# The four projections of u: four 32-column matmuls in place of one 128-column matmul

## The chip, the cores and the metric

One core of one Trainium2 chip. The metric is the device time of one execution in microseconds. The kernel before was timed in two runs: 3685.1 and 3701.43 us, median 3693.26 us.

## The reference

The input x is (4, 128, 96, 96): four images, 128 channels, fp32. Each is group-normalised (32 groups), read as a sequence of 9216 pixels in four orders (rows, rows backwards, columns, columns backwards), and each sequence goes through a gated state-space scan. The four results are put back into pixel order, mixed by `fuse_w`, and added to x. Cut to what matters here, for one sequence:

```python
t = grouped1x1(x, in_proj_w, in_proj_b, 4)         # 128 -> 512 channels, 4 groups of 32
u, gate = t[:, :256], t[:, 256:]
u = depthwise_conv(silu(u), dw_w)                  # 5 taps along the sequence
s = conv1x1(u, ssm_in_w)                           # 256 -> 32, and so are the next three
a = 0.999 + 0.0009 * sigmoid(conv1x1(u, ssm_delta_w, ssm_delta_b))
b = tanh(conv1x1(u, ssm_b_w, ssm_b_b))
c = tanh(conv1x1(u, ssm_c_w, ssm_c_b))
prefix = cumsum(log(clip(a, 0.0001, 0.9999)))
h = exp(prefix) * cumsum(b * s * exp(-prefix))
u = u + conv1x1(c * h + d * s, ssm_out_w)          # 32 -> 256
y = out_proj(grouped1x1(u * sigmoid(gate), mix_w, mix_b, 4))
```

The four projections of u are s, b, c and a's argument (delta): 32 channels each, together 128.

## The kernel before

Each image has two phases: V (pixels taken by columns) and H (by rows). In a phase silu(in_proj(groupnorm(x))) lies whole in SBUF, and two passes go over it, one for each direction. A pass walks 20 chunks of whole lines: 18 of 5 lines (480 pixels) and 2 of 3 lines (288 pixels). 4 images x 2 phases x 2 passes x 20 chunks make 320 steps, and all of it is fp32.

A step has these pieces, by function and line:

- `conv_and_gate`: the depthwise convolution. Channels 0 to 127 on TensorE as five matmuls with diagonal weights (L249, tile pc, copied to u by ScalarE at L265); channels 128 to 255 on ScalarE (first tap, L260) and VectorE (four taps, L262). Then the gate: two matmuls with 32 rows each (L271, tile pg, on rows 64 to 95 and 96 to 127), and their sigmoid (L275, tile gv).
- `scan`: the projections pp of u (L288), one matmul with 128 output columns for each half of u's channels, the second half (j = 1) first. The weights are laid out s, b, c, delta in groups of 32 columns, so that the result's partitions 0 to 31 hold s, 32 to 63 b, 64 to 95 c and 96 to 127 delta. ScalarE takes tanh of b (L293, tb), sigmoid of delta (L295, a) and tanh of c (L299, z); GpSimd scales and clips a (L301, L302); VectorE multiplies b and s (L303), runs the recurrence (L309, h), and makes z (L318, L319).
- `ssm_out`: z goes through two matmuls with 32 rows (L325 into pc, L329 into pz), and VectorE adds and gates (L330 to L332).
- `accumulate`: the folded output weights times gv (L340, tile py, two 128x128 matmuls), added to acc by VectorE (L345 in phase V).
- `front`: for the chunks of the next phase, during the second pass of a phase: normalisation, two matmuls with 32 rows (L225, tile pu, on rows 0 to 31 and 32 to 63), sigmoid (L229) and silu (L232).

The loop at the end runs the steps with one step's distance: `conv_and_gate` of step n, `ssm_out` of step n-1, `front` of a chunk where one is due, `scan` of step n, `accumulate` of step n-1. The framework keeps roughly this order on each engine, moves some instructions in the first chunks, and sets the waits from the data that instructions share. Each engine works through its own queue in that order. Tiles u, gv, tb, a, z and h have two buffers each, as do pc (`ps_u`) and pp (`ps_p`) in PSUM; pz and py have one.

So an ordinary step of the first pass stands in TensorE's queue as: L249 (5 matmuls), L271 (2), L325, L329, L288 (2), L340 (2). In second passes the two of L225 stand between L329 and L288.

## Time and profile before

| | |
|---|---|
| runs | 3685.1 and 3701.43 us, median 3693.26 |
| profiled execution: its span, first to last instruction | 3681.5 us (the page gives no other time for it; the runs lie 3.6 and 19.9 us above) |
| TensorE matmuls, busy | 3543.3 us, 9032 records |
| TensorE weight loads, busy | 1550.5 us, 9032 records |
| VectorE, busy | 2937.6 us |
| ScalarE, busy | 1572.0 us |
| GpSimd, busy | 393.2 us |
| mean granted clock of TensorE | 0.938 |
| DMA over the span | 25 GB/s |

How to read it: PE is TensorE's matmuls, PEld its weight loads, which overlap them; DVE is VectorE, ACT ScalarE, POOL GpSimd. A group in the page is one source line on one engine: the output tile, the tiles it reads, the count, then busy time in us and the mean length of one in ns, then the idle time of the engine just before those instructions and what ended most of it. A timeline row is start in us, length in us, engine, line, operation, tiles, count, and in brackets the idle time ahead and its releaser. The ends of matmuls are modelled, so distances between starts tell more than lengths. PEclk is the share of TensorE's full clock that was granted.

### The profile page before, as it was taken

To read this page: it belongs to the slowest core of one execution; us is meant where nothing else is said; L and a number is where in the kernel's file an instruction comes from. 1 tells how busy PE (TensorE), PEld (TensorE's weight loads), DVE (VectorE), ACT (ScalarE), POOL (GpSimd) and SP (SyncE) were. 2 spreads that over 40 slices of the span, in tenths; PEclk is the share of its full clock that TensorE was granted. 3 is DMA by queue.
4 is the path that set the end of the run, shared out by engine and by line. 5 is a ranking of instruction groups with operands and counts; after the bars stand their busy time and mean duration, and the time that the engine had idled before them with its cause. 6 is when DMAs were issued, how large, how long until landed. Compare 5 with 4: busy or idle time off the path is not lost.

```text
span 3681.5 us, 27637 instructions
## 1 busy us (share of the span) xinstructions
PE 3543.3 (96%) x9032; PEld 1550.5 (42%) x9032; DVE 2937.6 (80%) x4442; ACT 1572.0 (43%) x2572; POOL 393.2 (11%) x653
## 2 busy tenths in 40 slices
PE   7999999999999999999999999999999999999999
PEld 3334444444443444444443444444444344444444
DVE  7788887788877888778887788777887778877777
ACT  3334444444443444444443444444444444444443
POOL 0011111111111111111111011111111111111111
PEclk8899999999999999999999999999999999999999
DMA  4210000002100000001210000000121000000000
GB/s 145 82 37 12 19 22 0 0 30 65 59 3 0 17 19 17 0 0 46 65 45 0 0 20 22 11 0 3 59 62 32 0 4 21 22 6 0 3 24 25
DMA packets 56625, 92.14 MB, mean 25 GB/s; under 512 B 7296, under 2 KB 56352, under 8 KB 56480
## 3 DMA queue, kind: packets, MB, share of 16 engines
q1 hardware_dynamic: 54720, 89.68, 8.0%
q8 instruction: 70, 1.15, 0.1%
q10 hardware_dynamic: 1760, 0.70, 0.1%
q14 instruction: 75, 0.61, 0.1%
HBM read 71.48 MB, written 18.87 MB: 25 GB/s over the span
## 4 chain that ended last, share of the span: by engine, by line
DVE 46%; PE 41%; issue 6%; ACT 4%; DMA 2%; POOL 0%; ACTq 0%; DVEq 0%; POOLq 0%
DVE u L262 12%; PE pp L288 8%; PE pc L325 8%; PE pc L249 8%; DVE h L309 8%; PE py L340 6%; PE pz L329 6%; DVE z L319 5%; DVE tb L303 4%; DVE z L318 4%; DVE gv L332 3%; PE pu L225 3%; DVE u L331 3%; DVE sil L232 3%; ACT u L260 2%
## 5 line engine op out<-in xcount | busy, mean ns | idle before, releaser
L249 PE MATMUL pc<-sil,diag 128*128 128x480 f32 (+1 forms) x3200 | 1299.5, 552 | 0.0
L262 DVE SCALAR_TENSOR_TENSOR u<-sil,w_dw,u 128x480 f32<-128x480 f32 (+1 forms) x1280 | 889.0, 695 | 135.4 <-ACT u L260 124.0
L249 PEld LDWEIGHTS pc<-sil,diag 128*128 128x128 f32 x3200 | 610.7, 191 | 643.3 <-issue 624.7
L288 PE MATMUL pp<-u,w_proj 128*128 128x480 f32 (+1 forms) x1280 | 705.2, 680 | 3.1 <-DVE u L262 2.0
L265 ACT COPY u<-pc 128x480 f32<-128x480 f32 (+1 forms) x320 | 173.8, 543 | 1074.9 <-PE pc L249 1074.8
L340 PE MATMUL py<-gv,w_fin 128*128 128x480 f32 (+1 forms) x1280 | 614.2, 605 | 0.9
L301 POOL TENSOR_SCALAR a<-a 32x480 f32<-32x480 f32 (+1 forms) x320 | 189.8, 593 | 3252.3 <-ACT a L295 3252.3
L330 DVE TENSOR_TENSOR gv<-pc,gv 128x480 f32<-128x480 f32 (+1 forms) x320 | 203.8, 637 | 343.5 <-PE pc L325 337.1
L275 ACT ACTIVATE gv<-pg,b_in 128x480 f32<-128x480 f32 (+1 forms) x640 | 379.2, 642 | 143.8 <-PE pg L271 133.4
L325 PE MATMUL pc<-z,w_so 32*128 32x480 f32 (+1 forms) x640 | 332.6, 599 | 101.8 <-DVE z L319 100.5
L340 PEld LDWEIGHTS py<-gv,w_fin 128*128 128x128 f32 x1280 | 282.6, 222 | 331.4 <-issue 234.6
L288 PEld LDWEIGHTS pp<-u,w_proj 128*128 128x128 f32 x1280 | 244.3, 212 | 390.2 <-issue 273.8
L260 ACT ACTIVATE u<-sil,w_dw 128x480 f32<-128x480 f32 (+1 forms) x320 | 216.8, 678 | 404.7 <-DVE gv L332 398.0
L309 DVE TENSOR_TENSOR_SCAN h<-a,h,tb 32x480 f32<-32x480 f32 (+1 forms) x304 | 354.7, 1167 | 1.1
L271 PE MATMUL pg<-xn,w_in 32*128 32x480 f32 (+1 forms) x1280 | 345.5, 600 | 0.6 <-ACT gv L275 0.6
L229 ACT ACTIVATE sg<-pu,b_in 128x480 f32<-128x480 f32 (+1 forms) x320 | 201.7, 638 | 274.8 <-PE pu L225 274.7
L329 PE MATMUL pz<-z,w_so 32*128 32x480 f32 (+1 forms) x640 | 301.1, 550 | 0.0
L225 PE MATMUL pu<-xn,w_in 32*128 32x480 f32 (+1 forms) x640 | 264.2, 632 | 9.1 <-DVE sil L232 7.7
L293 ACT ACTIVATE tb<-pp,b_proj 32x480 f32<-32x480 f32 (+1 forms) x320 | 204.0, 637 | 150.8 <-PE pp L288 145.1
L303 DVE TENSOR_TENSOR tb<-pp,tb 32x480 f32<-32x480 f32 (+1 forms) x320 | 198.9, 621 | 70.3 <-ACT z L299 67.3
L232 DVE SCALAR_TENSOR_TENSOR sil<-pu,b_in,sg 128x480 f32<-128x480 f32 (+1 forms) x320 | 219.0, 691 | 24.9 <-ACT sg L229 23.5
L331 DVE TENSOR_TENSOR u<-pz,u 128x480 f32<-128x480 f32 (+1 forms) x320 | 203.9, 637 | 43.7 <-PE pz L329 2.6
(54 smaller groups left out, 2122.3 us busy)
## 6 DMA issues: line engine op xcount, KB each, us to landing
xn<-in_xv SPq DMA_DIRECT2D x72, 240.0 KB, 2.6
acc<-in_xh SPq DMA_DIRECT2D x72, 240.0 KB, 2.8
xn<-in_xh SPq DMA_DIRECT2D x72, 240.0 KB, 2.6
out<-res SPq DMA_DIRECT2D x72, 240.0 KB, 2.0
xs<-in_xh SPq DMA_DIRECT2D x54, 240.0 KB, 2.6
xn<-in_xv SPq DMA_DIRECT2D x8, 144.0 KB, 2.4
acc<-in_xh SPq DMA_DIRECT2D x8, 144.0 KB, 2.4
xn<-in_xh SPq DMA_DIRECT2D x8, 144.0 KB, 2.1
```

What stands on the lines that cost most here:

```text
L225: nc.tensor.matmul(pt[:, :n], w_in[q, :], xn[q, span(c)], start=True, stop=True)
L232: nc.vector.scalar_tensor_tensor(sil[:, j, bass.ds(PAD + STARTS[c] * WW, n)], pts[j][:, :n], b_in[:, j : j + 1], sg[:, :n], ALU.add, ALU.mult,
L249: nc.tensor.matmul(pu[:, :n], diag[:, w, :], sil[:, 0, bass.ds(o + k, n)], start=(k == 0), stop=(k == K - 1),)
L262: nc.vector.scalar_tensor_tensor(u[:, 1, :n], src, coef, u[:, 1, :n], ALU.mult, ALU.add)
L271: nc.tensor.matmul(pg[:, :n], w_in[q, :], xn[q, span(c)], start=True, stop=True)
L275: nc.scalar.activation(gv[:, j, :n], pgs[j][:, :n], AF.Sigmoid, bias=b_in[:, 2 + j : 3 + j])
L288: nc.tensor.matmul(pp[:, :n], w_proj[:, j, :], u[:, j, :n], start=(j == 1), stop=(j == 0))
L303: nc.vector.tensor_mul(tb[:, :n], s, tb[:, :n])
L309: nc.vector.tensor_tensor_scan(dirn(h), dirn(a), dirn(tb), 0.0 if st["first"] else carry[0], ALU.mult, ALU.add,)
L325: nc.tensor.matmul(pu[:, :n], w_so[:, 0:P], z[:, :n], start=False, stop=True, skip_group_check=True)
L329: nc.tensor.matmul(pz[:, :n], w_so[:, P:HID], z[:, :n], start=True, stop=True)
L340: nc.tensor.matmul(py[:, :n], w_fin[:, d, j, :], gv[:, j, :n], start=(j == 0), stop=(j == 1))
```

## The change

In `scan`, the one matmul for each half of u's channels becomes four, one for each group of 32 output columns. Each reads the same u (128 partitions, all pixels of the chunk), its own 32 columns of the weights, and writes its own 32 partitions of pp. In the built program such a matmul is placed on a tile of 128 rows by 32 columns of the array, at column 0, 32, 64 or 96. The order is: half 1 with its four tiles, then half 0 with its four tiles. `skip_group_check` switches off a check of the framework on the start and stop flags of groups that share a PSUM bank. Comments were taken out as well; from the changed place on, a line of the changed kernel has a number higher by 7.

```diff
         for j in (1, 0):
-            nc.tensor.matmul(
-                pp[:, :n], w_proj[:, j, :], u[:, j, :n], start=(j == 1), stop=(j == 0)
-            )
+            for q in range(4):
+                r = slice(MH * q, MH * (q + 1))
+                nc.tensor.matmul(
+                    pp[r, :n],
+                    w_proj[:, j, r],
+                    u[:, j, :n],
+                    start=(j == 1),
+                    stop=(j == 0),
+                    skip_group_check=True,
+                )
```

## The prediction

> **What bounds the kernel now.** I read the page from the shares down, then its chain, then the instructions of one step, then who waits for whom. On the page:

> ```profile
> PE 3543.3 (96%) x9032; PEld 1550.5 (42%) x9032; DVE 2937.6 (80%) x4442; ACT 1572.0 (43%) x2572; POOL 393.2 (11%) x653
> ...
> PEclk8899999999999999999999999999999999999999
> ...
> DVE 46%; PE 41%; issue 6%; ACT 4%; DMA 2%; POOL 0%; ACTq 0%; DVEq 0%; POOLq 0%
> ...
> L288 PE MATMUL pp<-u,w_proj 128*128 128x480 f32 (+1 forms) x1280 | 705.2, 680 | 3.1 <-DVE u L262 2.0
> ...
> L325 PE MATMUL pc<-z,w_so 32*128 32x480 f32 (+1 forms) x640 | 332.6, 599 | 101.8 <-DVE z L319 100.5
> ```

> TensorE is busy 96% of the 3681.5 us span, and the only idle time worth naming ahead of a matmul is 101.8 us before L325, until VectorE's z (L319). TensorE sets the pace, VectorE follows closely (80%, and 46% of the chain, because the chain hops over to it at each z). L288, the line that changes, has 1280 records for 320 chunks x 2 halves: an fp32 matmul leaves two, each with a weight load of its own. I call them its two passes. One ordinary step in the timeline of TensorE:

> ```profile
> 2010.67 4.19 PE L249 MATMUL pc<-sil,diag 128*128 128x480 f32 x10
> 2014.79 1.07 PE L271 MATMUL pg<-xn,w_in 32*128 32x480 f32 x4
> 2016.17 1.07 PE L325 MATMUL pc<-z,w_so 32*128 32x480 f32 x2 [0.31 <-DVE z L319]
> 2017.08 0.96 PE L329 MATMUL pz<-z,w_so 32*128 32x480 f32 x2
> 2017.97 1.88 PE L288 MATMUL pp<-u,w_proj 128*128 128x480 f32 x4
> 2019.69 1.77 PE L340 MATMUL py<-gv,w_fin 128*128 128x480 f32 x4
> 2021.30 2.98 PE L249 MATMUL pc<-sil,diag 128*128 128x480 f32 x7
> ```

> Ends are modelled, so I use starts. py's four passes run from 2019.69 to 2021.30: 1.61 us, 0.4025 a pass. pp's four take 1.72 (2017.97 to 2019.69), 0.11 over that; pz's two take 0.89, 0.085 over theirs. So going from the 32-row tiles of pz to the whole array costs 0.085 us ahead of the first pass and 0.11 behind its start, where its weight load isn't hidden: 0.195 us a change of tile shape.

> **Two tiles do run at once.** pg is two 32-row matmuls, on rows 64 to 95 and 96 to 127. Its instructions in the window from 2014.5 to 2015.0, and in that from 2015.5 to 2015.8:

> ```profile
> L271 PE MATMUL pg<-xn,w_in x2: 665/665/665, 2014.8 to 2014.8; 32*128 32x480 f32 x2
> ```

> ```profile
> L271 PE MATMUL pg<-xn,w_in x2: 561/561/561, 2015.3 to 2015.3; 32*128 32x480 f32 x2
> ```

> Two passes start together, and 0.5 us later the other two. The built program has each matmul's two passes one behind the other, first matmul complete before the second; so the second tile's first pass overtook the first tile's second pass. Four passes took two slots.

> **The clock is a second bound.** The table by stretches of time:

> ```profile
> 2003.40:2006.80 3.40, 2.96 (x7) 1.39 (x8) 2.06 (x4) 1.16 (x2) 0.00 (x0) 0.97 0.00 0
> 2006.80:2010.20 3.40, 3.40 (x5) 1.39 (x5) 1.74 (x3) 2.50 (x4) 0.44 (x1) 0.53 0.01 2
> ```

> PEclk (third from the right) is about half in the second stretch, behind one that held the z wait and four quarter-height passes. I cut the trace into stretches of 3.413 us at the clock's own changes, and in each summed the passes, weighted by the rows they use (32 of 128 counts a quarter). Full-clock stretches followed by half clock, 98 of them, had at most 0.39 of the array in use; the 924 others at least 0.37, and 5% of them under 0.44. About 0.38 is the limit. 119 of 1043 stretches run at half, some 203 us lost. This decides what an inefficient pp would cost.

> [...]

> **The change, part by part.** Each 128-column matmul becomes four of 32 columns over all 128 rows and all 480 pixels; in the built program they carry tile shape 128x32 at columns 0, 32, 64, 96, so the change does what it says. Records go from 9032 to 12872. A 32-column pass streams the same 480 columns, so it costs 0.4025 us too: the array work can at best stay equal, four tiles at once.
> 1. Passes. If four tiles overlap as pg's two do: 2 halves x 2 passes x 0.4025 = 1.61 us, as before: 0. Not shown for columns; the bounds are the rivals below.
> 2. Entry. Before, pp is entered by a shape change (from pz or, in second passes, from L225's 32-row tiles); after, also: 0. Its exposed load is 32 columns, not 128: if the four load side by side the 0.11 falls to an estimated 0.03 [...], if in turn it stays. 0 to -26 us over 320; I take -13.
> 3. Exit. New: py behind pp was the same shape, now it is another: +0.195 x 320 = +62 us at full clock, /0.938 (mean clock) = +66.
> 4. Cover. The exit's drain lies behind pp's end, and z's work starts at pp's end (tanh and sigmoid L293 to L299, L301/L302, the scan), so where PE then waits for z the drain comes out of that wait: up to 0.195 x 230 waits = 45 us. But acc (L345) needs py and stands in VectorE's queue ahead of tb (L303); where it comes late, tb, scan and z do too and the cover is gone (0). I take -22.
> 5. Clock. A gap of 0.195 us in 3.413 lowers the use by up to 0.057; stretches between 0.38 and 0.44 then fall under the limit, at most 5% of 924, some 40, at half of 3.413, 1.7 us, each: 0 to +68; I take +34.
> 6. Waits and queues. The first tile of each half carries the wait on u, the fourth raises the count for itself and its neighbours; L293 waits for the fourth, as it waited for the whole. Nothing new waits. PE's queue gets 32 instructions (loads and passes) for pp instead of 8; pg's two first passes start 7 ns apart in the trace's records, so I cost their issue at 0. Without that cover the staggered rival's price below bounds it. ScalarE, GpSimd and the DMA queues keep their order; VectorE's moves slightly in the first chunks alone: 0. The longer program adds 0.5 MB of instructions to 25 GB/s: hidden, DMA engines are idle most of the time.

> Sum: -13 + 66 - 22 + 34 = +65 us on 3681.5, span 3746.5. The runs' median is 3693.3, 11.8 above that span, so 3758 us (+1.8%). All low ends: -26 + 66 - 45 = -5; all high: +134. Own range of this case 3700 to 3830. It straddles 2% (3767), about what a measurement of this kernel can tell from no change.

> **The rivals.**
> Staggered or half rate (22%). Columns share the rows; if passes issue in program order, each tile's second pass blocks the next tile, 9 slots instead of 4: 9 x 0.4025 = 3.62 us, +2.01. If four streams of u from the same partitions get half the rate: +1.61. With 32 of 320 steps narrower (288 pixels) the mean is 0.96 of it: +495 to +617 us, with the exit 4250 to 4380. The array is then in use 0.45 to 0.5 in pp, beside a stretch at 0.25: about one more half-clock stretch a step, 320 x 1.7 = +545: to 4900, more where half begets half: 5400. For: [...] fp32 has two passes a tile. Against: pg's overtaking.

> Serial, the case on the other side (13%). Tiles of one row group don't overlap at all: 16 x 0.4025 = 6.44, +4.83 x 0.96 x 320 = +1480, 5240; at 0.25 of the array for 8 us a step at least two stretches go half, +1090: 6300. It decides from a second pass slot on: one extra slot of 0.4 us a half is already +247 us, 6.7%. [...]

> Dear changes of shape (5%): if a column shape's switch costs three times the row shape's, +125 more: 3880.

> Faster (3%): if the clock's limiter counted four small passes as more work than one large, the 203 us of half clock go: 3540. Nothing in the trace says so; otherwise no term is negative enough.

> **How the numbers follow.** Likeliest 57%: 3758. About 0.42 of it lies over 3767: 0.24, with the slow rivals' 0.40 makes slower 0.64; same 0.33; faster 0.03. Range for 8 in 10: from 3700 (leaves out faster and the likeliest's low tail, some 0.06) up to 5400, which takes in staggered and half rate with the clock's share, and leaves out most of serial (0.12).

> **What will show it.** Right: four L288 passes starting within some ns of each other, pp from first start to py's first start about 1.8 us, a gap of some 0.09 before py and 0.11 behind its first pass, mean clock 0.92 to 0.94, z wait below 100 us. Wrong: L288 passes 0.4 us apart one by one (serial), pairs in a staircase (staggered), passes 0.8 us apart (half rate), or a mean clock under 0.85.

## The result, and the profile after

The changed kernel takes 3716.46 us (3713.41 to 3719.51, two runs) against 3693.26: 1.0063 of before, interval 1.0034 to 1.0092. Run again beside other kernels it took 1.0077 (1.0063 to 1.0091). The forecast of 3758 us gave the direction, but +65 us became +23 to +28. One of all the runs below, of the kernel before with three TensorE taps, took 16293 us, and neither its time nor its profile is used.

The page of the changed kernel: engine shares, granted clock, chain, and two groups (the last column is the idle time ahead).

```profile
PE 3603.4 (97%) x12872; PEld 1417.5 (38%) x12872; DVE 2950.2 (79%) x4442; ACT 1571.7 (42%) x2572; POOL 393.0 (11%) x653
...
PEclk8899989999999998999999999899999999899999
...
PE 61%; DVE 32%; issue 4%; ACT 2%; DMA 2%; ACTq 0%; SPq 0%; DVEq 0%
...
L290 PE MATMUL pp<-u,w_proj 128*32 128x480 f32 (+1 forms) x5120 | 698.9, 663 | 2.0 <-DVE u L262 2.0
...
L332 PE MATMUL pc<-z,w_so 32*128 32x480 f32 (+1 forms) x640 | 332.9, 599 | 79.6 <-DVE z L326 75.6
```

pp has four times the passes and no more busy time (698.9 us): the tiles overlap. The idle time before z's matmul fell from 101.8 to 79.6 us, so some of the change went into a wait that was there anyway. (The 128-column matmul had 705.2 us of busy time, in the prediction's lines.) The step that answers to the one shown in the prediction, in the timeline of TensorE:

```profile
2013.67 0.96 PE L336 MATMUL pz<-z,w_so 32*128 32x480 f32 x2
2014.57 1.82 PE L290 MATMUL pp<-u,w_proj 128*32 128x480 f32 x16
2016.32 1.88 PE L347 MATMUL py<-gv,w_fin 128*128 128x480 f32 x4
2018.03 1.37 PE L249 MATMUL pc<-sil,diag 128*128 128x480 f32 x3
```

pp to py is 1.75 us (1.72 before), py to the taps 1.71 (1.61 before). In pp's records within 2014.5 to 2014.9, and within 2015.2 to 2015.38, four passes start together each time:

```profile
L290 PE MATMUL pp<-u,w_proj x4: 590/590/590, 2014.6 to 2014.6; 128*32 128x480 f32 x4
```

```profile
L290 PE MATMUL pp<-u,w_proj x4: 566/566/566, 2015.0 to 2015.0; 128*32 128x480 f32 x4
```

The records have the four 7 ns apart, all first passes, then all second passes, though the program lists each tile's two passes together. Over all steps at full clock, from starts (medians), two gaps are new. From pp's last pass to py's first it is 0.496 us, 0.093 over a pass; I call that drain, though the records show its length and not what fills it. From py's first pass to its second it is 0.507, 0.104 over a pass; I call that exposed load, since py's first weight load starts with the first pass (2016.313 and 2016.315 us in this step) and not in an earlier one. pp's exposed load fell by 0.08, and the tiles' spacing adds 0.02. That is 0.137 us more TensorE time a step, 44 us over 320 steps: what steps 2 and 3 of the prediction said, to 9 us. But the kernel became slower by less than that.

### What sets a step

I measured each step from one start of L303 (tb's product on VectorE) to the next. In first passes at full clock the median step is 10.50 us in the H order and 10.83 in the V order, before and after alike. z's last instruction in three first-pass steps of the kernel before, then two of the changed kernel:

```profile
2442.45 0.70 DVE L319 SCALAR_TENSOR_TENSOR z<-pp,d_sb,z 32x480 f32<-32x480 f32 x1
2452.94 0.70 DVE L319 SCALAR_TENSOR_TENSOR z<-pp,d_sb,z 32x480 f32<-32x480 f32 x1
2463.44 0.70 DVE L319 SCALAR_TENSOR_TENSOR z<-pp,d_sb,z 32x480 f32<-32x480 f32 x1
```

```profile
2476.92 0.70 DVE L326 SCALAR_TENSOR_TENSOR z<-pp,d_sb,z 32x480 f32<-32x480 f32 x1
2487.42 0.70 DVE L326 SCALAR_TENSOR_TENSOR z<-pp,d_sb,z 32x480 f32<-32x480 f32 x1
```

The same 10.50, with 0.137 us more on TensorE. The chain of the kernel before shows why (start, length, who; a V-order step):

```profile
2016.17 1.07 PE pc L325 x2
2017.24 0.82 PE pz L329 x2
2018.08 0.67 DVE u L331
2018.77 0.67 DVE gv L332
2019.52 0.70 ACT u L260
2020.25 0.73 DVE u L262
2021.00 0.72 DVE u L262
2021.72 0.99 DVE acc L345
...
2026.23 0.72 DVE z L319
```

From z through two short matmuls to VectorE, over to ScalarE's first tap (it waits for u's buffer: 398.0 of the 404.7 us that ScalarE idles before L260 end with VectorE's L332), back to VectorE's taps, acc, tb, scan and z: this loop holds neither pp nor the taps on TensorE. The share of 96% hid that TensorE has slack in the first-pass steps that run at full clock.

**A second edit nobody wrote.** In the built programs VectorE's queue differs in some 105 steps of second passes: the framework's scheduler turned `tb, acc, scan, tap, z` into `acc, tb, tap, scan, z` (res stands for acc where the result is written out). A second-pass step before, then one of the changed kernel, in VectorE's timeline:

```profile
1735.49 0.64 DVE L303 TENSOR_TENSOR tb<-pp,tb 32x480 f32<-32x480 f32 x1
1736.06 0.70 DVE L354 SCALAR_TENSOR_TENSOR res<-py,b_fin,acc 128x480 f32<-128x480 f32 x1
1736.68 1.20 DVE L309 TENSOR_TENSOR_SCAN h<-a,h,tb 32x480 f32<-32x480 f32 x1
1737.81 0.68 DVE L262 SCALAR_TENSOR_TENSOR u<-sil,w_dw,u 128x480 f32<-128x480 f32 x1
1738.42 0.64 DVE L318 TENSOR_TENSOR z<-z,h 32x480 f32<-32x480 f32 x1
```

```profile
1741.93 0.71 DVE L361 SCALAR_TENSOR_TENSOR res<-py,b_fin,acc 128x480 f32<-128x480 f32 x1
1742.55 0.63 DVE L310 TENSOR_TENSOR tb<-pp,tb 32x480 f32<-32x480 f32 x1
1743.12 0.70 DVE L262 SCALAR_TENSOR_TENSOR u<-sil,w_dw,u 128x480 f32<-128x480 f32 x1
1743.74 1.20 DVE L316 TENSOR_TENSOR_SCAN h<-a,h,tb 32x480 f32<-32x480 f32 x1
1744.98 0.65 DVE L325 TENSOR_TENSOR z<-z,h 32x480 f32<-32x480 f32 x1
```

With the tap between scan and z, the two take 1.74 us (1736.68 to 1738.42). With the tap ahead, tap, scan and the wait for the scan's last value take 1.86 (1743.12 to 1744.98). Over the whole traces z follows directly on a scan of 480 in 23 steps before (1.233 us from start to start) and in 131 after: 108 x 0.12 = 13 us. And acc's wait for py now stands ahead of tb, while tb's own wait shrinks. VectorE's waits, before and after:

```profile
DVE tb L303 <- ACT z L299: 67.3, 68, 1.5
DVE acc L345 <- PE py L340: 44.5, 35, 2.2
```

```profile
DVE acc L352 <- PE py L347: 86.9, 63, 2.3
DVE tb L310 <- ACT z L306: 12.9, 18, 1.3
```

### The profile page after: what moved, and what is told of

Same layout as the page of the kernel before. It is cut to its first block, busy times and chain, and to the rows that moved or that the text cites. A ratio compares the mean times of both kernels' runs of the same rounds, so it can differ in the third digit from the quotient of the medians.

```text
span 3717.8 us, 35219 instructions
## 1 busy us (share of the span) xinstructions
PE 3603.4 (97%) x12872; PEld 1417.5 (38%) x12872; DVE 2950.2 (79%) x4442; ACT 1571.7 (42%) x2572; POOL 393.0 (11%) x653
## 3 DMA queue, kind: packets, MB, share of 16 engines
q8 instruction: 100, 1.64, 0.2%
## 4 chain that ended last, share of the span: by engine, by line
PE 61%; DVE 32%; issue 4%; ACT 2%; DMA 2%; ACTq 0%; SPq 0%; DVEq 0%
PE pc L249 17%; PE pp L290 12%; PE py L347 10%; PE pc L332 8%; DVE u L262 7%; PE pz L336 6%; DVE h L316 5%; PE pg L271 4%; PE pu L225 3%; DVE z L326 3%; DVE acc L352 3%; DVE z L325 3%; DVE sil L232 2%; DVE tb L310 2%; DVE u L338 2%
## 5 line engine op out<-in xcount | busy, mean ns | idle before, releaser
L249 PE MATMUL pc<-sil,diag 128*128 128x480 f32 (+1 forms) x3200 | 1296.6, 551 | 0.0
L262 DVE SCALAR_TENSOR_TENSOR u<-sil,w_dw,u 128x480 f32<-128x480 f32 (+1 forms) x1280 | 890.6, 696 | 136.7 <-ACT u L260 125.2
L249 PEld LDWEIGHTS pc<-sil,diag 128*128 128x128 f32 x3200 | 608.3, 190 | 641.0 <-issue 623.2
L290 PE MATMUL pp<-u,w_proj 128*32 128x480 f32 (+1 forms) x5120 | 698.9, 663 | 2.0 <-DVE u L262 2.0
L347 PE MATMUL py<-gv,w_fin 128*128 128x480 f32 (+1 forms) x1280 | 636.0, 621 | 4.2 <-DVE gv L337 3.4
L347 PEld LDWEIGHTS py<-gv,w_fin 128*128 128x128 f32 x1280 | 242.6, 212 | 458.7 <-issue 138.7
L332 PE MATMUL pc<-z,w_so 32*128 32x480 f32 (+1 forms) x640 | 332.9, 599 | 79.6 <-DVE z L326 75.6
L260 ACT ACTIVATE u<-sil,w_dw 128x480 f32<-128x480 f32 (+1 forms) x320 | 216.6, 677 | 377.6 <-DVE gv L339 369.0
L271 PE MATMUL pg<-xn,w_in 32*128 32x480 f32 (+1 forms) x1280 | 340.8, 600 | 0.0
L290 PEld LDWEIGHTS pp<-u,w_proj 128*32 128x32 f32 x5120 | 150.2, 120 | 453.9 <-issue 436.8
L225 PE MATMUL pu<-xn,w_in 32*128 32x480 f32 (+1 forms) x640 | 272.1, 651 | 6.3 <-DVE sil L232 4.3
L352 DVE TENSOR_TENSOR acc<-py,acc 128x480 f32<-128x480 f32 (+1 forms) x160 | 165.2, 1032 | 87.0 <-PE py L347 86.9
```

The lines of the kernel that those rows point to most:

```text
L225: nc.tensor.matmul(pt[:, :n], w_in[q, :], xn[q, span(c)], start=True, stop=True)
L249: nc.tensor.matmul(pu[:, :n], diag[:, w, :], sil[:, 0, bass.ds(o + k, n)], start=(k == 0), stop=(k == K - 1),)
L262: nc.vector.scalar_tensor_tensor(u[:, 1, :n], src, coef, u[:, 1, :n], ALU.mult, ALU.add)
L271: nc.tensor.matmul(pg[:, :n], w_in[q, :], xn[q, span(c)], start=True, stop=True)
L290: nc.tensor.matmul(pp[r, :n], w_proj[:, j, r], u[:, j, :n], start=(j == 1), stop=(j == 0), skip_group_check=True,)
L332: nc.tensor.matmul(pu[:, :n], w_so[:, 0:P], z[:, :n], start=False, stop=True, skip_group_check=True)
```

## The experiments

All ratios are to the kernel before, run beside each on the same chip. "Lost" is half of the time at half clock, worked out from the clock and span of each timed run and averaged (235 to 237 us before). It measures how much half clock there was, not what it cost. "Order" is VectorE's in second passes. An interval of a pair is given with ±.

| kernel | ratio (interval) | lost, us | order |
|---|---|---|---|
| changed, again | 1.0077 (1.0063 to 1.0091) | 241 | changed |
| half 0 whole | 1.0044 (1.0028 to 1.0060) | 236 | of before |
| half 1 whole | 1.0194 (1.0177 to 1.0210) | 263 | of before |
| all in tiles | 1.0013 (1.0002 to 1.0023) | 227 | of before |
| pp and py in tiles | 1.0029 (1.0020 to 1.0038) | 229 | of before |
| changed, order kept | 1.0031 (1.0016 to 1.0045) | 231 | of before |
| before, order swapped | 1.0021 (1.0010 to 1.0032) | 240 | changed |
| 3 VectorE taps: before, changed | 0.9462, 0.9481 (each ± 0.002) | 144, 127 | see text |
| padded: before, changed | 0.9656, 0.9719 (± 0.002) | 29, 28 | of before, changed |
| padded, changed, order kept | 0.9676 (0.9654 to 0.9697) | 24 | of before |
| 3 TensorE taps: before, changed | 1.0665, 1.0772 (± 0.002) | 638, 559 | a third, in both |
| 7 TensorE taps: before, changed | 1.0150, 1.0233 (± 0.003) | 69, 58 | of before, changed |
| padded, 4 TensorE taps: before, changed | 0.9851, 0.9881 (± 0.003) | 140, 107 | of before, changed |

### Where the change of shape stands

The changed kernel again.

> The changed kernel once more, on the chip of the three runs beside it. The theory (shape): the change costs one more change of tile shape a step, behind pp (0.093 us drain and 0.107 us of exposed load), saves most of pp's exposed first load (0.107 to 0.028 us), and the wait for z gives part of it back: 1.004 to 1.009 of before, half-clock stretches within some 10 of the 119 of before. Rival one (clock): the gaps bring more half-clock stretches each time, so their count stands well above 119 again. Rival two (instruction count): the 3840 added passes cost by their number.

1.0077, as the shape theory had it. The profile has 128 half-clock stretches against 119 before and 126 in its first profile; over the timed runs 241 us were lost to half clock against 235. So at most a small part is the clock's. The count of passes is tested below.

Half 0 as one whole matmul (half 1 whole is its mirror image):

```diff
         for j in (1, 0):
+            if j == 0:
+                nc.tensor.matmul(pp[:, :n], w_proj[:, 0, :], u[:, 0, :n], start=False,
+                                 stop=True, skip_group_check=True)
+                continue
             for q in range(4):
```

> Half 1 of pp as four column tiles, half 0 as one whole matmul: the change of shape back comes between the halves, ahead of pp's end, instead of behind it. Shape theory with the z wait as cover: as many changes of shape as in the changed kernel, but none behind pp's end, so the z wait can't hide it: +0.115 us a step on pp, 320 x 0.115 x 1.066 = +39 us, and no cover: ratio 1.010 to 1.014. If the cover is no cover: as the changed kernel, 1.006. Instruction count: half of the changed kernel's cost, 1.003.

> Half 1 whole, half 0 as four column tiles: two changes of shape more than before, one into the tiles inside pp (0.093 + 0.028 us) and one out of them behind pp (0.2 us), and the long load at pp's entry stays. Shape theory: 320 x 0.32 x 1.066 = +109 us, less up to 45 us of cover: 1.017 to 1.030. Instruction count: the same as half 0 whole, 1.003.

Half 1 whole came as the shape theory has it: 1.0194, +72 us. TensorE now exceeds VectorE's loop: first passes 10.60 and 11.03 us. Half 0 whole didn't: 1.0044, cheaper than the changed kernel, where 1.010 to 1.014 was expected with the z wait as cover. pp to py takes 1.852 us there and py 1.610, together what they take in the changed kernel (1.747 and 1.714), so TensorE's time is equal and only the place differs. That speaks against my cover, "z's work starts at pp's end": z waits for VectorE's loop. But this kernel also kept VectorE's order of before, so it doesn't settle that alone.

py (and in the other kernel L249 too) in tiles, with the same inner loop over q:

```diff
-            nc.tensor.matmul(
-                py[:, :n], w_fin[:, d, j, :], gv[:, j, :n], start=(j == 0), stop=(j == 1)
-            )
+            for q in range(4):
+                r = slice(MH * q, MH * (q + 1))
+                nc.tensor.matmul(py[r, :n], w_fin[:, d, j, r], gv[:, j, :n],
+                                 start=(j == 0), stop=(j == 1), skip_group_check=True)
```

> Every 128-row matmul of the steps (the taps, pp and py) as four column tiles: over 16000 passes more than the changed kernel, but no change of shape that before didn't have, and a shorter exposed load at pp's entry. Shape theory: 320 x 0.06 to 0.08 x 1.066 = 20 to 27 us less than before: 0.993 to 0.997. Instruction count: 1.02 or more. Clock: as before, since no gap is added: 0.995 to 1.0.

> The changed kernel with py as four column tiles too: the change of shape moves from ahead of py to behind it (ahead of the taps), and TensorE's work stays the same to 0.03 us a step. If the cost is TensorE's own time in steps without slack: as the changed kernel, 1.006 to 1.009. If it comes through acc, which waits for py in VectorE's queue (70 us of waits before, 136 after): acc comes 0.2 us earlier again and most of it goes, 1.001 to 1.004.

All in tiles: 1.0013, so 17280 added passes (13440 over the changed kernel, fewer than I had written) cost next to nothing, and the instruction count is out. But the 20 us that TensorE saves didn't arrive either (0.993 to 0.997 was expected): its gap ahead of z's matmul grew from 172 to 197 us (from starts, with 0.4025 us a pass and twice that at half clock), which fits VectorE's loop. py in tiles: 1.0029 with the same TensorE time. That pointed to VectorE, though not, as I expected, through acc's lateness alone: these kernels all kept the order of before.

### VectorE's loop, and TensorE's slack

The last VectorE tap left out (`elif k < K - 1` in place of `else` at L262):

> The kernel before without the last of VectorE's four taps for channels 128 to 255, which leaves out that part of the convolution. Theory now (VectorE's loop): in first passes at full clock a step takes 10.50 us (H) or 10.83 us (V) in before, after and all tiles alike, because the loop z, L325, L329, VectorE's u and gv, ScalarE's first tap, VectorE's taps, acc, tb, scan, z sets it, and TensorE has slack there. With one tap of 0.70 us gone TensorE sets first passes too, at about 10.2 us: first passes 40 to 90 us shorter, ratio 0.975 to 0.99. Rival (TensorE sets all steps, VectorE only brings noise): 0.995 to 1.0.

> The changed kernel with the same tap left out. VectorE's loop theory: the slack that hid the change in first passes is gone, so each first-pass step pays 0.137 us more than its partner before (10.2 to 10.34 us at full clock), 160 x 0.137 = 22 us on top of the second passes' 25: 40 to 55 us over the partner, 1.011 to 1.015 of it, against 1.007 to 1.008 with all taps. Rival (TensorE sets all steps already): the difference to the partner stays at 25 to 29 us, 1.007 to 1.008.

For the kernel before both forecasts of the gain were too small. First passes at full clock go to 10.00 and 10.34 us in both kernels, still VectorE's loop: TensorE isn't the bound at 10.2, since L325 starts beside L271 when z comes early (in one step of the kernel before, L271 at 1727.75 us and L325 at 1727.76). The total falls by 198 us, and 92 us less are lost to half clock. So VectorE, not TensorE, is what first-pass steps at full clock wait for. The pair differs by 0.0019 only, under both forecasts. It isn't a clean pair: the changed kernel loses 17 us less to half clock. z follows directly on the scan in both, so the order can't act through the scan's wait here.

Fewer and more taps on TensorE (`taps[1:4]`; or two more matmuls into pc with a weight tile of zeros):

> The kernel before without TensorE's first and last tap (three of five matmuls at L249 remain), which leaves out that part of the convolution: 1.61 us of TensorE's work less a step, VectorE's work untouched. VectorE's loop theory: first-pass steps at full clock keep their 10.50 and 10.83 us, second passes stay near 11.4; only steps with half clock gain: ratio 0.965 to 0.99. Rival (TensorE sets the pace, as predicted): 320 x 1.61 x 0.96 = 495 us less, 0.865 to 0.89.

> The changed kernel with the same two taps left out. VectorE's loop theory: the added change of shape lies in TensorE's slack in nearly every step, so it costs 0 to 8 us over its partner, 1.000 to 1.002. Rival (TensorE sets the pace): the 0.137 us a step stay on the path whatever the length of the taps: 40 us or more over the partner, 1.010 to 1.014.

> The kernel before with two more taps of zero weights on TensorE (seven matmuls into pc; the result is unchanged): 1.61 us more TensorE work a step. Both theories have TensorE as the bound here. VectorE's loop theory: the first part of it fills the slack, so less than 320 x 1.61 x 0.96 = 495 us is added: 1.04 to 1.09. Rival (TensorE sets the pace already): 1.11 to 1.14.

> The changed kernel with the same two added taps. With TensorE as the bound in every step the whole price of the change shows: 320 x 0.137 us = 44 us at full clock, 44 to 52 over its partner, 1.011 to 1.014 of it, about twice what it cost the kernel before. If the price had been hidden by something else than slack on TensorE: 1.006 to 1.008 of the partner as before.

With two taps fewer, full-clock first passes stay at 10.40 and 10.82 us (changed kernel's profile), as VectorE's loop says, yet both kernels are slower than before, at a lower clock (changed kernel; 0.936 with all taps):

```profile
core 0: 3978.8 us, clock 0.859
```

With less array use there was more half clock: 638 and 559 us lost. The pair differs by 0.0107, about 40 us: the rival forecast that (1.010 to 1.014 of the partner), and mine of 0 to 8 us missed. With so much half clock, and unequal in the two, the pair doesn't tell what a step with slack pays. With two taps more the clock rises to 0.984 (0.938 in the profile of the kernel before) and the total by 1.5% only, under my 4 to 9%. There TensorE does set first passes: 10.87 us, and 11.01 in the changed kernel; second passes go from 12.42 to 12.56. That 0.14 is the price of the change of shape where nothing hides it. The pair differs by 0.0083, some 31 us (expected 44 to 52), order included.

### The clock

z and its weights padded with zeros to 128 rows, so that L325 and L329 use the whole array in the same number of passes:

```diff
-    w_so = load(ssm_out_wT, [MH, HID], "w_so")
+    w_so = wp.tile([P, HID], F32, name="w_so")
+    nc.gpsimd.memset(w_so, 0.0)
+    nc.scalar.dma_start(w_so[0:MH, :], ssm_out_wT)
+    zbuf = [wp.tile([P, CW], F32, name=f"zb{i}") for i in range(2)]
+    for t in zbuf:
+        nc.gpsimd.memset(t, 0.0)
...
-        z = wk.tile([MH, CW], F32, tag="z", name=f"z_{id_}")
+        z128 = zbuf[st["i"] % 2]
+        z = z128[0:MH, :]
...
-        st["z"] = z
+        st["z"] = z128
```

> The kernel before with z and its weights padded with zero rows from 32 to 128, so that L325 and L329 use all rows of the array at the same number of passes; nothing of the result changes. Clock theory (a 3.413 us stretch with less than 0.38 of the array's rows in use is followed by half clock): nearly all half-clock stretches go, mean clock over 0.98. Against it stand one more change of shape in second passes (160 x 0.2 = 32 us) and L225's overlap with pz, which is lost (160 x 0.25 = 40 us). First passes fall to VectorE's 10.50 and 10.83 us, second passes lose some 139 - 72 us: ratio 0.95 to 0.975. Rival (the clock follows idle time only, not rows): half clock as before, ratio 1.005 to 1.02.

> The changed kernel with the same padding. Now a column-tile shape stands between two whole-array matmuls. If the clock's share of the change's cost is real, it goes here: first passes as the padded kernel before (VectorE's loop), second passes 160 x 0.14 = 22 us over it: 1.005 to 1.009 of the padded kernel before, 0.955 to 0.985 of before. If the clock were no part of the cost, the difference would be the same as between the kernels without padding, 1.007 to 1.008.

```profile
core 0: 3569.5 us, clock 0.990
```

3568.43 us, 0.9656 of before: with more rows in use 7 half-clock stretches are left in place of 119, as the prediction's limit, counted from the trace, had it, and this version beats both kernels. First passes stay at 10.50 and 10.84 us. The change still costs 0.0063 of before here, 23 us, with the clock out of the way and losses to half clock equal: so the clock isn't what makes its price there. Nor is it TensorE's time in first passes. The matmuls ahead of pp use the whole array here, so the tiles add 0.335 us to a first-pass step (0.093 ahead of pp, 0.138 from pp to py, 0.104 from py to the taps, by starts), and the step's period stays.

One TensorE tap less on top, for slack in second passes:

> The padded kernel before without TensorE's last tap (four matmuls at L249 remain), which leaves out that part of the convolution: slack on TensorE in second passes too, and hardly any half clock. VectorE's loop theory: first passes keep 10.50 and 10.83 us; second passes fall from 11.56 to some 11.3 us; ratio 0.945 to 0.965. Rival (TensorE's work sets the time once the clock is full): 320 x 0.805 x 0.96 = 247 us less than the padded kernel, 0.90.

> The changed kernel with the same padding and the same tap left out. If slack is what hides the change, and half clock and second passes are where it is paid, it costs 0 to 8 us over its partner here, 1.000 to 1.002 of it. If it costs something that slack doesn't hide: 20 us or more, 1.005 and up, as with padding alone.

The clock fell again (0.962 against 0.990 with all taps; 140 us lost), so 0.9851 and not 0.945 to 0.965. The pair differs by 0.0030 with intervals as wide, and the losses are unequal, so it decides nothing by its total. Full-clock second passes of the H order take 11.53 us, as with all TensorE taps, so TensorE isn't their bound; in the changed kernel 11.66. The 0.13 us is the size of the changed order (0.12).

### The order and the tiles, each alone

The two orders were forced with edges between instructions of VectorE's queue; all other queues keep their order. In the changed kernel acc and res stand behind tb again (for i >= 3 of second passes that have a next phase):

```diff
+def after_on_engine(tc, ins, earlier):
+    tc.add_manual_dep(ins.ins, earlier.ins.name, mybir.DependencyInfo(
+        mybir.DependencyClass.NoSync, mybir.DependencyReason.DATA), reason="order")
...
-            nc.vector.tensor_add(
+            ins = nc.vector.tensor_add(
                 part, py[:, :n].rearrange("p (w h) -> p w h", h=HH), part
             )
+            if ordered:
+                after_on_engine(tc, ins, tb_ins[0])
             return
```

> The changed kernel with VectorE's queue put back to the order of before in second passes. In before, tb (L303) stands ahead of acc or res, which wait for py, and the scan follows at once; in the changed kernel the framework's scheduler has put acc or res ahead of tb and a tap ahead of the scan, in some 105 second-pass steps; the kernel with py in tiles kept the order of before. All other queues are as in the changed kernel. Order theory (most of the price is this order): 1.001 to 1.004 of before. Rival (the change of tile shape on TensorE is the price): 1.006 to 1.009, as the changed kernel.

In the kernel before, `accumulate(prev)` is issued from within `scan`, ahead of L303, and L303 is put behind it:

```diff
+        done = accumulate(early) if early is not None else None
-        nc.vector.tensor_mul(tb[:, :n], s, tb[:, :n])
+        ins = nc.vector.tensor_mul(tb[:, :n], s, tb[:, :n])
+        if done is not None:
+            after_on_engine(tc, ins, done)
```

> The kernel before with VectorE's queue in the order of the changed kernel in second passes: acc or res ahead of tb, a tap ahead of the scan. pp stays one matmul, TensorE's queue is that of before. Order theory: slower without any tile, 1.003 to 1.006 of before; the two parts together make the 1.007 to 1.008 of the changed kernel. Rival (tile shape alone): 0.999 to 1.001.

> The padded changed kernel with VectorE's order of before in second passes, hardly any half clock. The padded pair stands at 0.9656 (whole pp) and 0.9719 (tiles, changed order). Order theory: most of the gap closes, 0.965 to 0.969. Rival (tile shape): 0.971 to 0.973.

The tiles with the old order cost 1.0031, 11 us. (Their order isn't wholly that of before: 39 of 320 steps, most of them where passes meet, still differ.) The new order without any tile costs 1.0021, 8 us, under the 1.003 to 1.006 that I expected. From the changed kernel (1.0077) to the kept order it is 0.0046, 17 us. So the order takes 8 us alone and 17 on top of the tiles, the tiles 11 alone and 20 (1.0077 less 1.0021) on top of the order. Half 0 whole and py in tiles, which have the same TensorE time as the changed kernel and the order of before, fit the tiles alone (1.0044 and 1.0029).

The padded kernels separate the two best, since hardly any half clock is left. By total it is 0.9656, 0.9676 and 0.9719: 7 us for the tiles (the intervals overlap), 16 for the order. By step it is plainer. Second-pass steps of the H order in VectorE's timeline: the padded kernel before, the changed one with the order kept, the changed one:

```profile
1697.10 0.64 DVE L309 TENSOR_TENSOR tb<-pp,tb 32x480 f32<-32x480 f32 x1
1708.62 0.64 DVE L309 TENSOR_TENSOR tb<-pp,tb 32x480 f32<-32x480 f32 x1
1720.15 0.64 DVE L309 TENSOR_TENSOR tb<-pp,tb 32x480 f32<-32x480 f32 x1
```

```profile
1697.40 0.64 DVE L326 TENSOR_TENSOR tb<-pp,tb 32x480 f32<-32x480 f32 x1
1708.93 0.64 DVE L326 TENSOR_TENSOR tb<-pp,tb 32x480 f32<-32x480 f32 x1
1720.46 0.64 DVE L326 TENSOR_TENSOR tb<-pp,tb 32x480 f32<-32x480 f32 x1
```

```profile
1696.59 0.64 DVE L316 TENSOR_TENSOR tb<-pp,tb 32x480 f32<-32x480 f32 x1
1708.24 0.63 DVE L316 TENSOR_TENSOR tb<-pp,tb 32x480 f32<-32x480 f32 x1
1719.90 0.64 DVE L316 TENSOR_TENSOR tb<-pp,tb 32x480 f32<-32x480 f32 x1
```

The medians are 11.53, 11.52 and 11.66 us (V order: 11.89, 11.86, 12.00), and first passes have 10.50 and 10.83 or 10.84 in all three. So in padded steps at full clock the tiles cost nothing and the order costs 0.11 to 0.14 us in each second-pass step.

Without padding the parts don't simply add up. I took the ordinary steps of the profiles, from L303 of a pass's fourth step to that of its eighteenth. In the seven second passes that feed a next phase these take 1205.6 us before. They take 1209.3 with the tiles alone and 1215.6 with the order alone, but 1231.8 and 1227.3 in the two profiles of the changed kernel: 4 and 10 us each alone, 22 to 26 together. Half-clock stretches in them: 60, 59, 63, 66 and 64. First passes show no clear cost (1238, 1244, 1243, 1238 and 1238). The steps in between, where passes meet, take 926 us before, 941 with the tiles alone, 923 with the order alone, and 937 and 944 in the changed kernel: there the tiles cost 11 to 18 us. These are single executions, and the timed runs of one kernel lie up to 34 us apart, so the split is rough.

## Why the prediction missed

Step by step, in its own terms:

- **1, passes: right.** Four column tiles of fp32 overlap, passes 7 ns apart; neither the staggered nor the serial rival occurred. Their chances, 22% and 13%, were the author's estimates: the trace of before has no column tile. Nor does it hold these tiles up that all four share the rows: each tile's second load (2014.594 us for the first) starts beside running passes (from 2014.568 on), as pp's second load did before (2018.078, beside a pass from 2017.972 on).
- **2 and 3, entry and exit: right in size.** 0.137 us a step, 44 us (said: -13 + 66 = 53, clock included). The entry's load fell from 0.104 to 0.02 us (0.03 was the author's estimate, a quarter of the 0.11 for a quarter of the columns; nothing of before showed how a load's time goes with its columns).
- **4, cover: wrong in mechanism and too small.** "z's work starts at pp's end" puts pp on the path to z. In first passes at full clock the loop that sets the step holds neither pp nor py, and all of the 0.137 us is hidden (with padding, all of 0.335). Tiles cost 11 us of 44 alone and 20 on top of the order, so 24 to 33 were covered where 22 were said. That the z wait on the page fell by 22 us is no support: it is one sum over all kinds of steps. Behind this step stands the opening claim, "TensorE sets the pace": the profile's 46% of the chain on VectorE and a fixed 10.50 us spoke against it.
- **5, clock: mis-sized.** +34 was said. The profiles lost 239 and 242 us against 228 (with the set-up, which the prediction's 203 leaves out), but that profile of before lost less than most of its runs; over the timed runs it is 241 against 235, some 6 us. The added gap came largely out of the z wait, so the array's gaps in total hardly moved (370 us before, 375 after, counted as above), and few stretches sank under the limit. The limit of 0.38, counted by rows, was borne out by the padded kernels: 7 half-clock stretches in the one of before. Its "924 others" are all full-clock stretches, the 98 among them; the others are about 830, which changes nothing.
- **6, queues: wrong.** "VectorE's moves slightly in the first chunks alone: 0". It moves in 105 steps of second passes, which costs 8 us alone and 17 on top of the tiles, of 28 measured; in the padded kernels it is 16 of 23. ScalarE's queue moves too, about the changes of pass. The longer program shows as 1.64 MB of instructions on queue q8 of the page, 1.15 before: the 0.5 MB said.

So two errors of opposite sign stood in the sum: 65 us for the tiles, where 11 were paid alone and 20 on top of the order, and 0 for the order, where 8 to 17 were. All signs listed as "Right" came (pp to py 1.75 us, gaps of 0.09 and 0.10 us, clock 0.936, z wait 79.6 us), though the sum was far off: they test the tiles, and none of them tests what sets a step.

What stays open: the two parts alone (0.0031 and 0.0021) add up to 0.0052, the changed kernel has 0.0077; the difference of 0.0025 is about as large as the three intervals together (0.0023). The profiles point to a real remainder, in second passes with half clock, but nothing shows how it comes about. Nor is it shown why the tiles cost something where passes meet, and which of that is due to the other queues that move there. How far the order acts through the scan's wait (13 us by count) and how far through acc ahead of tb wasn't separated.

## What to carry to other kernels

A busy share of 96% isn't a bound: measure the step's period before and after, and find the loop that has it. When an edit changes the number of instructions on one engine, compare the queues of all engines over the whole program, since a scheduler may re-sort another engine's, as it did here in some 105 steps. And before taking work off TensorE, see what that does to its clock: here 1.61 us less a step came with 0.84 in place of 0.936.
